# A new hand-written order for the first stage of a Flamingo block: loads, steps and the engines of its conversions

## The chip, the cores and the metric

The kernel runs on one core of a Trainium2 chip. The metric is the device time in microseconds (us) of one execution; lower is better. The core has a matrix engine (TensorE, called PE in the profile), three engines for element-wise work (VectorE or DVE, ScalarE or ACT, GpSimd or POOL), and SyncE (SP), which here issues nearly all DMA transfers. Each engine works through its own queue of instructions strictly in order, and an instruction that waits for another engine holds everything behind it on its own.

## The reference

Two batches of 512 tokens with 1024 features (`x`) and two contexts of 1024 x 1024 (`ctx`) come in. The first half of the block is an "attention" without a softmax: the normalised tokens and the context are each put on an integer grid of 256 steps, and multiplied.

```python
def fake_quant(x, s, z):
    q = clip(round(x / s + z), 0, 255)
    return (q - z) * s

x = x + tanh(g_xattn[0]) * (fake_quant(layernorm(x)) @ fake_quant(ctx))
x = x + tanh(g_ffn[0]) * ffn(layernorm(x))
```

`ffn` is a shared gated layer, `(silu(x @ sw1 + sb1) * (x @ sw2 + sb2)) @ sw3 + sb3`, with 512 inner features, plus experts of the same form with 256 inner features, of which a router (`x @ router_w`, a softmax, and the best two within the two best of four groups) picks two of 16 for each token.

## The kernel before

The 1024 tokens are eight tiles of 128; tiles 0 to 3 belong to batch 0 and tiles 4 to 7 to batch 1. The context of a batch has eight row blocks of 128. The work up to the first part of the shared layer is written out by hand as one long list of small steps, `START`, which a loop turns into instructions one after another. The order of the list is the order of every engine's queue; the tile framework adds the waits between engines. The loads ahead of it stand in a second list, `LOADS`, and all go through SP in that order.

```python
LOADS = "x.1 x.3 c.0 c.1 c.2 c.4 c.3 x.2 c.5 x.4 c.6 c.7.0 c.7.1 b x.5 w.0.0 w.1.1 w.1.0 w.0.1"
for step in START.split():
    name, *args = step.split(".")
    do[name](*(int(a) if a.isdigit() else a for a in args))
```

In `LOADS`, `x.t` is a token tile (512 KB), `c.k` a context block of batch 0 (512 KB; `c.7` comes in two halves), `b` the biases, `w.c.i` the weights of inner block c of the shared layer (i is 0 for `sw1`, 1 for `sw2`), 512 KB in rows of 128 numbers. `x.0` is loaded first, in two halves. In the profile, `X` is a token tile, `cr` a context block, and `sa0r`, `sb0r`, `sa1r`, `sb1r` are `w.0.0`, `w.0.1`, `w.1.0`, `w.1.1`.

A step names its operation, its tile or block, sometimes a half, and often the engine:

- token side, tile t: `bn` and `ag` take mean and variance (DVE, L205, L209); `qa`, `qp`, `qr` make scale and offset (`qp` is a power on POOL, L218); `qn` turns a sign for ACT; `q8` quantises to bytes (DVE L237, ACT L235); `qc` centres to bf16 (L190 on ACT, L192 elsewhere); `qt` transposes on PE (L248) into `pq`; `qe` copies that out into `qT`.
- context side, batch b, block k: `c8` quantises (ACT L261, others L263) and `cc` centres into `cq` (L190, L192). In the text c1.k is the load of block k of batch 1.
- `mm.t.k` multiplies transposed block k of tile t by context block k, into two accumulators `at` (PE, L273, two products of 512 columns; `mm.t.7.0` is one of them).
- `e` adds the result to the tile (DVE, L285); `sq` squares on ACT (L294); `fm`, `fc`, `fa`, `fr` make the second norm's mean and scale; `fn` applies it into `xn` (DVE, L323); `px` transposes on PE (L328); `xh`, `xl` split the transpose into a high part `XH` (L184, L186) and a low part `XL` (DVE, L338); `xc` makes a negated copy for the router (ACT).
- shared layer, weights `w.c.i`: `wh` takes the high part and `wl` the low part (L589); `um` is eight products of 256 columns on PE (L598) into `sp`; `us` and `ug` apply the gate (ACT L605, DVE L608).
- `ld` issues the eight context blocks of batch 1 and then `x.6` and `x.7`; `lw` issues three small DMAs for the router, its weights `rwf` (64 KB, L617), a bias `rb` of 16 numbers (L618) and a broadcast row `rbi` (L619); `xd` stores a tile, `lz` loads the next two weight blocks, `ud` stores a gated block. All of these are on SP.
- `kb.n` is n dummy products on PE (L570) ahead of the first real ones; `pw` makes four sums for the router on POOL (L672).

PSUM has six banks of one kind (`at`, `sp`, and `px` with `.m`) and two of another (`pq` and `px` without it); `q8`, `qc`, `c8` and the gated blocks rotate over seven buffers of SBUF. A step that needs a bank or a buffer waits for the last reader of the one that it takes over.

After `START` come the rest of the shared layer (L385), the router, the experts (L429) and the down projection (L978, L989), in which PE works from product to product.

Of the kernel before, what the change touches and what calls it, by code (L numbers as in the profile page):

```python
# [74 lines left out]


# [1173 lines left out]
```

## Time and profile before

| | |
|---|---|
| median of 3 runs | 307.93 us (307.24 to 308.5) |
| the profiled execution | 308.13 us |
| its span, first to last instruction | 306.4 us |
| PE busy | 296.7 us, 97% of the span |
| DVE, ACT, POOL busy | 217.4, 150.4, 88.3 us |
| the granted clock of TensorE | 0.999 of full speed |
| first PE instruction of the stage after `START` | 79.38 us after the span's start |

A line of a group or of the timeline has the engine, the line of the kernel, the operation, its output and inputs, shapes and types, and how often it came; in brackets, the idle time ahead of it and what ended that. A line of the waits tells who waited for whom: us in total, how often, the longest. A line of the chain has start, duration and what it was. "SPq" is SP's own queue of DMA issues: its durations are those of the issue, not of the transfer.

### The profile page before, as it was taken

To read this page: it belongs to the slowest core of one execution; us is meant where nothing else is said; L and a number is where in the kernel's file an instruction comes from. 1 tells how busy PE (TensorE), PEld (TensorE's weight loads), DVE (VectorE), ACT (ScalarE), POOL (GpSimd) and SP (SyncE) were. 2 spreads that over 40 slices of the span, in tenths; PEclk is the share of its full clock that TensorE was granted. 3 is DMA by queue.
4 is the path that set the end of the run, shared out by engine and by line. 5 is a ranking of instruction groups with operands and counts; after the bars stand their busy time and mean duration, and the time that the engine had idled before them with its cause. 6 is when DMAs were issued, how large, how long until landed. Compare 5 with 4: busy or idle time off the path is not lost.

```text
span 306.4 us, 4242 instructions
## 1 busy us (share of the span) xinstructions
PE 296.7 (97%) x1502; PEld 232.4 (76%) x1502; DVE 217.4 (71%) x371; ACT 150.4 (49%) x214; POOL 88.3 (29%) x118
## 2 busy tenths in 40 slices
PE   8889999999999999999999999999999999999993
PEld 3344794599858888888888888888888888888882
DVE  3999998996948599864572758725489597756522
ACT  2779999768252464453241544417663638420000
POOL 2567996659322312400011110212430050000000
PEclk9999999999999999999999999999999999999999
DMA  6999950982159972641504209049999999812222
GB/s 229 418 395 313 393 190 1 279 356 88 35 159 193 216 154 43 120 158 38 170 0 120 86 4 254 18 149 360 286 348 314 346 216 300 255 74 103 81 93 75
DMA packets 39553, 56.90 MB, mean 186 GB/s; under 512 B 5389, under 2 KB 22613, under 8 KB 39524
## 3 DMA queue, kind: packets, MB, share of 16 engines
q1 hardware_dynamic: 36194, 48.16, 45.6%
q0 software_dynamic: 3328, 8.39, 14.7%
q8 instruction: 14, 0.23, 0.3%
q14 instruction: 15, 0.12, 0.1%
q10 hardware_dynamic: 2, 0.00, 0.0%
HBM read 39.76 MB, written 12.59 MB: 171 GB/s over the span
## 4 chain that ended last, share of the span: by engine, by line
PE 81%; DMA 11%; SPq 3%; DVE 1%; POOL 1%; issue 0%; POOLq 0%
PE pb L978 11%; DMA X<-in_dram 9%; PE sp L385 7%; PE pa L978 7%; PE pc L978 6%; PE sp L598 4%; PE b2B L429 3%; PE b3B L429 3%; PE b7B L429 3%; PE b5B L429 3%; PE b4B L429 3%; PE b6B L429 3%; PE at L273 3%; DMA cr<-in_dram 2%; PE b6C L429 2%; PE b7C L429 2%
## 5 line engine op out<-in xcount | busy, mean ns | idle before, releaser
L273 PE MATMUL at<-cq,qT 128*128 128x512 bf16 x128 | 29.9, 379 | 1.3 <-POOL cq L192 1.0
L273 PEld LDWEIGHTS <-qT 128*128 128x128 bf16 x128 | 12.2, 98 | 14.9 <-issue 2.1
L989 DVE SCALAR_TENSOR_TENSOR Y<-pb,tg,Y 128x512 f32<-128x512 f32 x12 | 9.0, 749 | 8.6 <-PE pb L978 8.5
L825 POOL DMA_DIRECT2D xf<-xf x8 | 7.2, 938 | 23.3 <-DMA xf<-xf 13.4
L949 POOL DMA_DIRECT2D rS<-hrouted x6 | 7.3, 1601 | 21.9 <-DMA rS<-hshared 15.1
L570 PE MATMUL pz<-zero 128*128 128x512 bf16 x43 | 11.6, 421 | 1.5 <-DVE zero L563 1.5
L989 DVE SCALAR_TENSOR_TENSOR Y<-pc,tg,Y 128x512 f32<-128x512 f32 x8 | 5.9, 750 | 10.0 <-PE pc L978 10.0
L205 DVE BATCH_NORM_STATS2 st<-X 128x6 f32<-128x512 f32 x16 | 10.4, 675 | 3.5 <-DMA X<-in_dram 3.5
L461 POOL TENSOR_TENSOR b4s<-b4s,gates 128x512 f32<-128x512 f32 x2 | 2.6, 1288 | 35.1 <-ACT b4s L471 27.9
L285 DVE SCALAR_TENSOR_TENSOR X<-at,cx_scale,X 128x512 f32<-128x512 f32 x16 | 11.7, 744 | 0.1
L294 ACT ACTIVATE xn<-X,s 128x512 f32<-128x512 f32 x16 | 11.5, 718 | 0.0
L261 ACT ACTIVATE q8c<-cr,sc_in,rs 128x1024 uint8<-128x1024 f32 (+1 forms) x9 | 10.2, 1135 | 2.0 <-DMA cr<-in_dram 2.0
L190 ACT ACTIVATE cq<-q8c,nz 128x1024 bf16<-128x1024 uint8 (+1 forms) x10 | 10.4, 1057 | 1.2 <-DVE q8c L263 1.1
L338 DVE TENSOR_TENSOR XL<-px,XH 128x512 fp32r<-128x512 f32 x16 | 10.3, 679 | 0.5 <-ACT xf L345 0.5
L184 ACT CAST XH<-px 128x512 fp32r<-128x512 f32 x13 | 7.3, 607 | 5.6 <-PE px L328 5.6
L598 PE MATMUL sp<-XH,sb 128*128 128x256 f32 x64 | 9.6, 291 | 0.0
L672 POOL TENSOR_TENSOR xf<-XH,XL 128x1024 f32<-128x1024 f32 x4 | 9.5, 2411 | 0.0
L972 DVE TENSOR_TENSOR rB<-rB,rB 128x1024 f32<-128x1024 f32 x8 | 9.2, 1219 | 0.0
L570 PEld LDWEIGHTS <-zero 128*128 128x128 bf16 x43 | 4.2, 105 | 6.4 <-DVE zero L563 1.5
L328 PE MATMUL px<-ident,xn 128*128 128x128 f32 x64 | 8.8, 274 | 0.3 <-DVE xn L323 0.3
L598 PE MATMUL sp<-XH,sa 128*128 128x256 f32 x64 | 8.8, 286 | 0.0
L598 PEld LDWEIGHTS sp<-XH,sb 128*128 128x128 f32 x64 | 8.3, 191 | 0.4 <-ACT XH L184 0.2
(602 smaller groups left out, 889.2 us busy)
## 6 DMA issues: line engine op xcount, KB each, us to landing
cr<-in_dram SPq DMA_DIRECT2D x15, 512.0 KB, 8.5
x_after<-X SPq DMA_DIRECT2D x8, 512.0 KB, 7.2
xf<-xf POOLq DMA_DIRECT2D x8, 512.0 KB, 5.2
rB<-in_dram SPq DMA_DIRECT2D x8, 512.0 KB, 8.8
Y<-x_after SPq DMA_DIRECT2D x8, 512.0 KB, 8.7
out_dram<-Y SPq DMA_DIRECT2D x15, 256.0 KB, 2.1
X<-in_dram SPq DMA_DIRECT2D x7, 512.0 KB, 9.4
rS<-hrouted POOLq DMA_DIRECT2D x6, 512.0 KB, 11.5
```

The source lines that it names most:

```text
L190: nc.scalar.activation(out, q8, AF.Identity, bias=nz)
L205: nc.vector.bn_stats(st_[t][:, h, :], X[t][:, half(h)])
L273: nc.tensor.matmul(acc[t][h], qT[b][:, t % TB, k, :], cq[b][k // KH][:, k % KH, half(h)], start=(k == 0), stop=(k == KD - 1))
L285: nc.vector.scalar_tensor_tensor(xs, acc[t][h], cx_scale, xs, ALU.mult, ALU.add, accum_out=sq_[t][0][:, h : h + 1])
L294: nc.scalar.activation(xn_[t][:, half(h)], X[t][:, half(h)], AF.Square, bias=s[:, h : h + 1], scale=-float(H), accum_out=q[:, h : h + 1],)
L338: nc.vector.tensor_tensor(XL[b][q][p], px_[t, q], XH[b][q][p].bitcast(F32), ALU.subtract)
L385: nc.tensor.matmul(p, wx[:, k, :], xx[b][k // KH][:, k % KH, cols], start=first and k == 0, stop=last and k == KD - 1,)
L429: nc.tensor.matmul(p, w[:, k, :], x[:, k, :], start=f and k == 0, stop=l and k == KH - 1, skip_group_check=not first,)
L570: nc.tensor.matmul(pz[0], zero[:, :P], zero, start=True, stop=True)
L598: nc.tensor.matmul(up_[c, lo, i], w[:, k, :], x[0][k // KH][:, k % KH, lo : lo + 256], start=p == 0 and k == 0, stop=p == 2 and k == KD - 1,)
L978: nc.tensor.matmul(p, x[:, ts(t, P)], w[:, cl], start=first and k == 0 and i == 0, stop=k == KH - 1 and i == 2, skip_group_check=not first,)
L989: nc.vector.scalar_tensor_tensor(X[t][:, cl], p, tgf, X[t][:, cl], ALU.mult, ALU.add)
```

## The change

Only the two lists change. Every step is still there once, with the same arithmetic, and the 43 dummy products are too.

- `LOADS`: `x.2` goes ahead of `c.2`, and `x.4` behind all of batch 0's context; `c.3`, `c.4`, `c.6`, `c.5` swap places; `w.1.0` comes first of the weights, and `x.5` and `b` stand among them.
- `START`: of PE's steps, the first products start on tiles 0 and 1 as before, but tile 2 comes before tile 3; nearly all dummy products stand in one run ahead of the first transpose.
- `lw` moves from the middle of batch 1 to the front of the list, ahead of `ld`. `ld` itself moves up to the first part of the list; both are still behind all of `LOADS` on SP. `xd.0`, `xd.1` and `lz` follow directly behind `ld`.
- Some 55 steps go to another engine: for example `qc.0` from ACT and DVE to POOL, `c8.0.1` from ACT to POOL, `qc.1` from DVE to ACT, `c8.0.4` and `cc.0.4` from ACT to DVE, both halves of `c8.0.7` and `cc.0.7` from DVE and ACT to POOL, `wh.1.1.1` from DVE to ACT, `c8.1.1` and `c8.1.2` from POOL to ACT, `c8.1.0` from ACT to DVE, `qc.4` from ACT to POOL, `c8.1.6` and `cc.1.5` from ACT to DVE.

The diff in full:

```diff
@@ -39,38 +39,38 @@
 LOWEST = -3.4028234663852886e38
 
 
-LOADS = "x.1 x.3 c.0 c.1 c.2 c.4 c.3 x.2 c.5 x.4 c.6 c.7.0 c.7.1 b x.5 w.0.0 w.1.1 w.1.0 w.0.1"
+LOADS = "x.1 x.3 c.0 c.1 x.2 c.2 c.3 c.4 c.6 c.5 c.7.0 c.7.1 x.4 w.1.0 w.0.0 x.5 b w.1.1 w.0.1"
 START = """
-kb.4 ks bn.0.0 bn.0.1 ag.0 qa.0.dve kr kn xx.0 qp.0 kb.8 kb.1 qr.0.dve kb.3 q8.0.dve.0 kx kz qc.0.act.0 stage.0 kb.7
-qt.0.0 bn.1.0 bn.1.1 bn.3.0 ag.1 bn.3.1 ag.3 qa.1.pool c8.0.0.act.0 qp.1 q8.0.dve.1 qa.3.dve qc.0.dve.1 cc.0.0.act.0
-kb.2 qr.1.pool c8.0.1.act c8.0.0.dve.1 cc.0.1.act kb.3 q8.1.dve qc.1.dve kb.7 qt.0.1 qe.0.dve.0 qp.3 kb.3 c8.0.2.act
-qr.3.pool kb.4 qt.1 q8.3.dve cc.0.0.pool.1 mm.0.0 qe.1.dve cc.0.2.pool c8.0.5.pool mm.0.1 qc.3.act qe.0.dve.1
-c8.0.3.dve kb.1 mm.1.0 mm.1.1 qt.3 cc.0.3.dve mm.1.2 bn.2.0 bn.2.1 c8.0.4.act qe.3.act mm.0.2 ag.2 cc.0.4.act bn.4.0
-bn.4.1 c8.0.6.dve mm.0.3 mm.3.0 cc.0.5.act mm.3.1 qa.2.pool qp.2 c8.0.7.dve.0 cc.0.7.dve.0 mm.1.3 cc.0.6.act mm.3.2
-mm.1.4 mm.3.3 mm.1.5 qr.2.pool c8.0.7.act.1 mm.0.4 mm.0.5 ld ag.4 pb q8.2.dve mm.1.6 qc.2.pool bn.5.0 cc.0.7.act.1
-mm.1.7.0 mm.0.6 bt mm.3.4 wh.0.0.0.act qa.4.dve mm.1.7.1 qt.2 e.1.0 mm.3.5 mm.0.7.0 e.1.1 mm.0.7.1 mm.3.6 sq.1.0
-qe.2.dve e.0.0 sq.1.1 wh.0.0.1.act qp.4 e.0.1 qr.4.pool bn.5.1 fm.1.pool sq.0.0 fm.0.dve ag.5 fc.1.pool fc.0.dve
-qa.5.dve mm.2.0 mm.2.1 wl.0.0.0.pool sq.0.1 mm.2.2 fa.1.pool wh.1.0.0.act fa.0.dve mm.2.3 mm.2.4 fr.1 wh.1.1.0.dve
-fn.1.0 fr.0 mm.2.5 mm.2.6 mm.2.7.0 mm.3.7.0 fn.1.1 px.1.0.m fn.0.0 px.1.1.m fn.0.1 qp.5 e.3.0 px.0.0 c8.1.0.act
-qn.4.dve mm.2.7.1 xh.1.0.act xh.1.1.act wh.1.1.1.dve xh.0.0.act xl.1.0 xl.1.1 c8.1.1.pool wh.0.1.0.dve px.0.1
-wh.0.1.1.dve xl.0.0 mm.3.7.1 wl.0.0.1.pool xh.0.1.act stage.1 q8.4.act xl.0.1 qc.4.act e.2.0 qr.5.pool c8.1.3.act
-um.1.0.1.0 um.0.0.0.0 wl.1.0.0.dve um.0.0.1.0 qt.4 e.3.1 wh.1.0.1.act um.0.0.1.1 c8.1.2.pool c8.1.4.pool q8.5.dve
-qe.4.dve cc.1.3.act e.2.1 cc.1.1.act wl.0.1.0.pool wl.0.1.1.dve cc.1.4.pool um.0.0.0.1 um.1.0.1.1 fm.3.pool um.1.0.0.0
-cc.1.0.pool um.0.0.0.2 qc.5.act bn.6.0 c8.1.6.act bn.7.0 bn.7.1 cc.1.2.act c8.1.7.act um.0.0.1.2 ag.7 qt.5 bn.6.1
-qa.7.dve c8.1.5.pool qe.5.dve us.0.0 ag.6 qa.6.dve um.1.0.0.1 qp.7 qr.7.pool mm.4.0 ug.0.0 lw mm.4.1 sq.2.0 cc.1.5.act
-qn.7.dve mm.4.2 mm.4.3 mm.5.0 mm.5.1 cc.1.6.dve mm.5.2 fm.2.pool mm.5.3 mm.4.4 fc.2.dve mm.5.4 q8.7.act sq.3.0
-wl.1.0.1.dve mm.5.5 qp.6 mm.5.6 cc.1.7.dve qc.7.act qr.6.pool mm.5.7 q8.6.dve qc.6.dve mm.4.5 qt.7 sq.2.1 e.5.0 qt.6
-fa.2.pool qe.7.act e.5.1 mm.4.6 mm.4.7 xd.5 fm.5.dve e.4.0 fr.2 mm.7.0 mm.7.1 fc.3.dve sq.3.1 fa.3.dve sq.5.0 fr.3
-qe.6.act e.4.1 mm.7.2 fm.4.pool mm.7.3 mm.7.4 mm.7.5 fn.3.1 sq.4.0 fn.2.1 fn.3.0 mm.7.6 sq.5.1 mm.6.0 fc.5.pool mm.6.1
-lz wl.1.1.0.dve mm.7.7 px.3.1 mm.6.2 xh.3.1.act fa.5.pool mm.6.3 fr.5 mm.6.4 px.2.1 fc.4.pool e.7.0 xd.1 mm.6.5 sq.4.1
-mm.6.6 rc xh.2.1.act fn.2.0 e.7.1 fm.7.pool fn.5.1 mm.6.7 fn.5.0 sq.7.0 xl.3.1 px.2.0.m e.6.0 px.3.0.m xd.0 fc.7.pool
-um.1.0.0.2 wl.1.1.1.pool sq.7.1 xh.3.0.act e.6.1 xx.1 sq.6.0 px.5.1.m xh.2.0.act fm.6.dve xc.5.1 xl.3.0 ud.0.0
-fc.6.pool px.5.0 um.1.0.1.2 xl.2.1 fa.4.pool sq.6.1 fr.4 um.1.256.0.0 fa.7.dve xh.5.1.act xl.2.0 um.0.256.0.0
-xh.5.0.dve fa.6.pool um.1.256.0.1 xl.5.1 fn.4.0 fr.7 fn.7.0 fr.6 px.4.0 us.1.0 px.7.0.m xh.7.0.act fn.7.1 xc.5.0 xd.4
-um.0.256.0.1 um.1.256.0.2 fn.4.1 us.1.256 px.4.1.m fn.6.1 fn.6.0 xd.2 px.6.0.m xc.7.0 xc.6.0 xc.4.0 xl.5.0 ug.1.0
-um.0.256.0.2 px.6.1 xh.6.1.dve xh.4.0.act xl.4.0 xl.6.1 um.1.256.1.0 xd.6 pw xl.7.0 xh.4.1.act xh.6.0.act um.1.256.1.1
-um.1.256.1.2 px.7.1 um.0.256.1.0 um.0.256.1.1 xd.7 xc.4.1 xc.6.1 ud.1.0 ug.1.256 um.0.256.1.2 xd.3 xh.7.1.dve us.0.256
-xl.4.1 xc.7.1 xl.6.0 xl.7.1 ud.1.256 ug.0.256 ud.0.256
+kb.4 ks bn.0.0 bn.0.1 kb.8 kb.1 ag.0 lw kx kr c8.0.0.act.0 c8.0.0.act.1 qa.0.pool qp.0 qr.0.dve kb.3 kz q8.0.dve.0
+kb.7 kn kb.2 bn.1.0 bn.1.1 ag.1 ld stage.0 qa.1.dve kb.3 kb.7 bn.3.0 qc.0.pool.0 qp.1 qr.1.dve c8.0.1.pool
+cc.0.0.act.1 q8.0.dve.1 qc.0.pool.1 kb.3 kb.4 q8.1.dve bn.3.1 bn.2.0 bn.2.1 qt.0.0 qc.1.act ag.2 qe.0.act.0
+cc.0.0.pool.0 c8.0.2.act qt.1 ag.3 qa.2.dve qe.1.dve c8.0.3.act mm.0.0 cc.0.1.dve qa.3.pool kb.1 cc.0.3.act qt.0.1
+cc.0.2.dve mm.1.0 qe.0.act.1 qp.2 mm.0.1 mm.1.1 qr.2.pool c8.0.4.dve q8.2.dve mm.1.2 qc.2.act mm.1.3 mm.0.2 qp.3
+c8.0.6.dve cc.0.6.act mm.0.3 cc.0.4.dve qr.3.pool c8.0.7.pool.0 cc.0.7.pool.0 qt.2 c8.0.5.dve c8.0.7.pool.1 mm.0.4
+mm.1.4 qe.2.dve mm.2.0 cc.0.5.act q8.3.dve mm.1.5 qc.3.act mm.1.6 mm.0.5 xx.0 bn.4.0 cc.0.7.pool.1 bn.4.1 wh.1.0.0.dve
+mm.1.7.0 e.1.0 wh.1.0.1.act qt.3 ag.4 mm.0.6 mm.0.7.0 qe.3.act sq.1.0 mm.0.7.1 qa.4.dve mm.2.1 wl.1.0.1.pool e.0.0
+e.0.1 mm.2.2 mm.1.7.1 qp.4 wh.0.0.0.act sq.0.0 sq.0.1 e.1.1 mm.2.3 mm.2.4 mm.2.5 qr.4.dve mm.3.0 wh.1.1.0.dve
+fm.0.pool mm.3.1 mm.3.2 fm.1.pool pb fc.0.dve qn.4.dve bn.5.0 wh.0.0.1.dve fc.1.pool fa.0.pool bn.5.1 sq.1.1
+wh.0.1.0.act mm.3.3 mm.3.4 bt fr.0 q8.4.act fn.0.0 mm.3.5 fa.1.pool px.0.0 fn.0.1 ag.5 fr.1 px.0.1 fn.1.1 mm.2.6
+mm.2.7.0 px.1.1.m fn.1.0 mm.2.7.1 xh.0.0.act c8.1.0.dve xh.0.1.act qa.5.pool px.1.0.m xh.1.1.act xh.1.0.act
+wh.0.1.1.dve e.2.0 wl.0.1.1.pool xl.1.1 mm.3.6 xl.0.1 xl.1.0 xl.0.0 qc.4.pool c8.1.2.act mm.3.7.1 qp.5 e.2.1
+wl.1.0.0.dve c8.1.1.act wl.0.1.0.dve sq.2.0 qr.5.dve c8.1.4.pool wh.1.1.1.act q8.5.dve xd.0 mm.3.7.0 um.1.0.0.0 e.3.0
+fm.2.pool um.0.0.1.0 qt.4 c8.1.3.act um.0.0.0.0 stage.1 e.3.1 bn.6.0 wl.0.0.0.pool wl.0.0.1.pool cc.1.4.act xd.1
+um.1.0.1.0 qe.4.dve cc.1.3.act bn.6.1 lz bn.7.0 cc.1.0.pool ag.6 um.1.0.0.1 sq.2.1 qa.6.dve um.1.0.0.2 cc.1.2.act
+um.0.0.1.1 bn.7.1 xd.3 ag.7 um.0.0.0.1 fc.2.dve um.0.0.1.2 qc.5.act qa.7.dve c8.1.5.pool c8.1.6.dve um.0.0.0.2
+cc.1.1.act cc.1.5.dve mm.4.0 qp.7 qt.5 qr.7.pool um.1.0.1.1 mm.4.1 c8.1.7.act qn.7.dve us.0.0 mm.4.2 mm.4.3 qe.5.dve
+sq.3.0 fa.2.pool mm.4.4 fr.2 qp.6 q8.7.act ug.0.0 mm.5.0 fn.2.0 qr.6.dve cc.1.7.dve mm.5.1 mm.5.2 qc.7.act q8.6.dve
+cc.1.6.dve mm.4.5 mm.5.3 rc mm.5.4 qt.7 qc.6.act fm.3.pool mm.4.6 sq.3.1 mm.4.7 wl.1.1.1.pool mm.5.5 wl.1.1.0.dve
+qe.7.dve qt.6 mm.5.6 e.4.0 e.4.1 us.1.0 fm.4.pool mm.5.7 e.5.0 mm.7.0 mm.7.1 sq.5.0 px.2.0.m mm.7.2 mm.7.3 fn.2.1
+fc.3.dve qe.6.dve xd.2 e.5.1 mm.7.4 px.2.1 sq.5.1 fa.3.pool mm.6.0 xh.2.0.act sq.4.0 fr.3 mm.7.5 mm.7.6 fm.5.dve
+fc.5.pool fn.3.0 mm.7.7 mm.6.1 fa.5.pool xh.2.1.act mm.6.2 fn.3.1 mm.6.3 fr.5 e.7.0 px.3.0.m mm.6.4 fn.5.1 xl.2.0
+px.3.1 xh.3.0.act mm.6.5 xh.3.1.act e.7.1 xl.2.1 sq.4.1 xx.1 fn.5.0 sq.7.0 px.5.1.m fm.7.pool sq.7.1 mm.6.6 fc.7.pool
+fc.4.dve px.5.0 xl.3.0 xl.3.1 xd.7 um.1.256.0.0 mm.6.7 fa.7.dve e.6.0 um.1.256.0.1 um.1.0.1.2 xc.5.1 fr.7 fa.4.pool
+um.0.256.1.0 fr.4 fn.7.0 sq.6.0 um.0.256.0.0 e.6.1 fm.6.dve xh.5.1.act ud.0.0 sq.6.1 fc.6.dve fn.4.0 px.7.0.m
+um.1.256.0.2 fn.4.1 xd.5 xl.5.1 fa.6.dve xc.5.0 px.4.0 px.4.1.m um.0.256.0.1 fr.6 fn.6.1 xd.6 xh.5.0.act us.1.256
+xh.4.0.act fn.6.0 fn.7.1 um.0.256.1.1 xc.4.0 xl.5.0 xh.4.1.dve px.7.1 xc.4.1 px.6.0.m ug.1.0 xl.4.0 pw xh.7.0.act
+um.0.256.0.2 xh.7.1.dve ud.1.0 xh.6.0.act xl.6.0 xc.7.1 um.1.256.1.0 px.6.1 xc.6.1 xl.7.1 xl.7.0 um.1.256.1.1 us.0.256
+xc.6.0 xh.6.1.dve xd.4 um.1.256.1.2 xl.6.1 ug.1.256 um.0.256.1.2 xc.7.0 ug.0.256 ud.0.256 ud.1.256 xl.4.1
 """
 
 
```

## The prediction

> **What bounds the kernel now.** I read the page first: busy shares, then the chain that ended last.
>
> ```profile
> PE 296.7 (97%) x1502; PEld 232.4 (76%) x1502; DVE 217.4 (71%) x371; ACT 150.4 (49%) x214; POOL 88.3 (29%) x118
> ...
> PE 81%; DMA 11%; SPq 3%; DVE 1%; POOL 1%; issue 0%; POOLq 0%
> ```
>
> TensorE is the bound; DMA holds the chain only early. So I asked for the waits of PE alone (total us, times, longest), then PE's timeline.
>
> ```profile
> PE pz L570 <- DVE zero L563: 1.5, 1, 1.5
> PE pq L248 <- DVE qx L192: 1.3, 3, 0.5
> PE at L273 <- POOL cq L192: 1.0, 1, 1.0
> PE px L328 <- DVE xn L323: 0.3, 1, 0.3
> PE pq L248 <- ACT qx L190: 0.2, 1, 0.2
> PE at L273 <- DVE sa L608: 0.2, 1, 0.2
> ```
> ```profile
> 16.63 0.81 PE L273 MATMUL at<-cq,qT 128*128 128x512 bf16 x3 [1.01 <-POOL cq L192]
> ...
> 31.81 1.63 PE L328 MATMUL px<-ident,xn 128*128 128x128 f32 x12 [0.27 <-DVE xn L323]
> ...
> 34.12 1.39 PE L598 MATMUL sp<-XH,sb 128*128 128x256 f32 x8
> ...
> 79.38 2.00 PE L385 MATMUL sp<-XH,sa 128*128 128x512 f32 x8
> ```
>
> START ends at 79.38; from there the chain is PE alone up to the last addition. In START, PE waits 1.5 for its first operand (untouched) and 3.0 in all the rest. The change keeps every PE step, the 43 dummy products too. So it can win at most 3.0 us, and loses what new waits exceed that. Last I read the chain's loads, the DMA by stretch (last numbers: clock, DMA share, GB/s), and SP:
>
> ```profile
> 26.61 6.14 DMA cr<-in_dram
> ...
> 32.77 11.19 DMA X<-in_dram
> ```
> ```profile
> 26.00:28.00 2.00, 2.00 (x17) 1.13 (x16) 1.94 (x6) 2.00 (x6) 1.71 (x7) 1.00 1.05 290
> ...
> 38.00:40.00 2.00, 2.00 (x19) 2.00 (x18) 2.00 (x4) 2.00 (x4) 2.00 (x2) 1.00 1.02 418
> 40.00:42.00 2.00, 2.00 (x19) 2.00 (x19) 2.00 (x5) 1.48 (x2) 2.00 (x2) 1.00 1.01 338
> 42.00:44.00 2.00, 2.00 (x21) 1.84 (x20) 1.69 (x5) 2.00 (x3) 1.90 (x5) 1.00 0.25 33
> ```
> ```profile
> 34.07 0.38 SPq L617 DMA_DIRECT2D rwf<-in_dram  x1
> 35.31 3.54 SPq L618 DMA_DIRECT2D rb<-in_dram  x1
> 38.90 1.12 SPq L619 DMA_DIRECT2D rbi<-in_dram  x1
> ```
>
> The load stream is full from 2 to 42 us: c1.1 lands at 32.75, x.7 at 43.96. Summing bytes of 2 us stretches, x.4 (eleven half-MB loads, 5.77 MB) has moved by 17.25 and lands at 19.20: landing is about 1.95 after moving. A load of 4 KB rows takes 1.25 (0.524 MB at 420 GB/s). From x.5 (7.38 MB, 21.3) to the fourth weight half (9.48 MB, 28.0) is 6.7 us, so a half takes 1.68.
>
> **The change, part by part.** I walk each engine's new queue in order with durations of the trace.
>
> *Loads.* x.2 moves up, x.4 down: x.2 lands at 12.95, c.7 at 20.4 (21.7 before), x.4 at 21.8, w.1.0 23.5, w.0.0 25.2, x.5 26.4, w.1.1 28.2, w.0.1 30.0. The total up to the second context is unchanged.
>
> *lw ahead of ld.* Three DMAs (64 KB router weights in rows of 64 bytes, 64 bytes of biases, one broadcast row) move past all eight c1 loads, x.6 and x.7, on SP and in the rings. Row: in 40:44 the 0.74 MB moved take until about 42.8; the 0.68 MB of large rows need 1.6 us from 40, so the small ones hold the engines about 1.2. [...] c1.2 lands at 35.6, x.6 near 43.8, x.7 at 45.2. SP's issue time is taken as hidden: SP comes to lw near 26.5, the rings are full of weights to 28.0; without that cover see the first rival.
>
> *First products.* PE runs 42 dummies in a row to 12.7 (0.217 each at the end). c8.0.0 goes whole to ACT (c.0 lands 10.46): two halves and cc.0.0's half at 0.72-0.81, to 12.7; qc.1 (1.15) follows to 13.8; qt.1 runs at 13.9, qe.0 on ACT (half of 1.01), first product 14.35 (15.24 before, its second half 16.63). New waits of PE up to qt.3: 1.0 for qc.1, then 0.1, 0.25 (cc.0.1 on DVE), 0.5 (cc.0.3 behind c.3, landed 15.45), 0.4 (qc.2), 0.45 (qe.2 behind c8.0.5), 0.1. qt.3 ends at 23.8; before, the same work was done at 24.1 (32 products and three transposes at 24.36; 3 x 0.217 less, one transpose of 0.44 more). Gain 0.3.
>
> *Swapped engines.* Some 55 small and large steps change engine, at like prices: a 1024-wide conversion is 1.06-1.23 on ACT, 0.75-0.81 on DVE, 1.1-1.33 on POOL. What can differ is DVE beside POOL:
>
> ```profile
> 18.26 1.57 DVE L192 TENSOR_SCALAR cq<-q8c,nz 128x1024 bf16<-128x1024 uint8 x1
> ...
> 47.62 0.74 DVE L192 TENSOR_SCALAR cq<-q8c,nz 128x1024 bf16<-128x1024 uint8 x1
> ```
>
> The first runs beside a POOL conversion (18.07 to 19.29), the second beside small POOL steps. POOL gets c8.0.1, qc.0, half of cc.0.0 and all of c.7; DVE gets c8.0.4 and c8.0.5. No stretch of before has this mix: between nothing and 0.8 for each of three overlaps. I take 0.3 in all, which goes into the waits below.
>
> *px.0.0.* PE comes to it at 29.7. On DVE before fn.0.0: e.0.0 from 24.6, three e at 0.75 to 26.85, qr.4, then wh.1.1.0 waits for w.1.1 (28.2); behind it fc.0, qn.4, two bn (0.61), wh.0.0.1, fn.0.0: px.0.0 at 31.2. New wait 1.5 (0.27 before). With w.1.1 early it would be 0.5. [...] First um at 34.8 instead of 34.12, where the first eight themselves run 0.3 slow: loss 0.4.
>
> *um.1.0.1.0, fourth of its kind.* It needs wh.1.1.1, moved to ACT behind c8.1.2, c8.1.1 and sq.2.0: 35.6 + 1.23 + 1.15 + 0.9 + 0.6 = 39.5. PE, after 0.5 for qt.4 (qc.4 now on POOL behind wl.0.1.1), is there at 38.8: wait 0.7. With the loads as before, wh.1.1.1 would end at 38.5: none. Seven um of 0.97 then lead to mm.4.0 at 46.3.
>
> *mm.5.0.* It needs qe.5 and banks that ug.0.0 frees. DVE: bn.6.0 waits for x.6, then qe.4, bn.6.1, bn.7, ag, fc.2, c8.1.6, cc.1.5 and qn.7 (behind qr.7 on POOL) stand before qe.5: 49.8, ug.0.0 50.3. PE is there at 49.85: wait 0.4 (0.2 before).
>
> *Buffers.* q8, qx and c8 rotate over seven buffers; I followed each reuse in the new order, and every earlier reader is done when the next writer comes (c8.0.5, the tightest, needs cc.0.2, done 1.5 earlier). Nothing; if one binds, its conversion is late by up to one of 0.8 to 1.2.
>
> *Later.* Transposes of tiles 2 to 7, their squares and the stores keep about one PE step of slack by the walk; xd.0, xd.1 and lz now stand on SP directly behind the loads and move by about 51 (four halves of a MB, 1.25 to 1.68 each, after 45), in rings that are idle from 42 to 53; the four POOL sums of pw (9.5) end near 82, needed at 86. Nothing, but see the third rival.
>
> Sum on PE from qt.3: -0.3 at the front, then waits of 1.5 + 0.5 + 0.7 + 0.4 = 3.1. Before had from there 0.27 + 0.19 + 0.32, 0.3 in the slow first um, and 0.15 of pipeline restart at each of three stops (a product of 512 columns counts 0.379 and they follow at 0.217): 1.5. With the new stops' restarts already in the starts: -0.3 + 3.1 - 1.5 = +1.3. Against the profiled execution (308.13, span 306.4) 309.4; it stands 0.2 over the median 307.93, so 309.2.
>
> **The rivals.**
>
> *SP is held (slower).* rb's issue took 3.54 and rbi's 1.12 behind rwf. If they take that in the new place as well, from 26.6, c1.0 is issued near 31.3; the rings run dry at 29.2, and it moves 2.5 later still. It decides once rb and rbi end later than about 28.7. c1.2, wh.1.1.1 and x.7 shift by 2.5 and PE has nothing else: +3.8, 311.7. For it: these rows. Against: in 35 to 39 the rings were full, and the two DMAs are tiny.
>
> *The front pays (faster).* w.1.1 lands by 27.2 and lw costs near its bytes: px.0.0 waits 0.5, wh.1.1.1 and x.7 cause nothing. Then 1.0 + 0.7 + 0.3 go from the sum: -0.7, 307.2; with the overlaps at nothing and the early waits halved, -2.0. For it: earlier c.7 and tile 2. Against: before is within 3.0 of its floor.
>
> *A stop near the end (slower).* xh.2.0 now stands on ACT behind sq.5.1, and px.3.0 needs a bank from e.7.0 or xl.2.0: slack 0.4. If it is gone, one or two stops of 0.8 are added: 310.5.
>
> **How the numbers follow.** Main course 0.55, SP held 0.17, the front pays 0.20, late stop 0.08. 0.5% is 1.54 us, about what a measurement of this kernel can tell from no change. The main course, 1.3 with 1.0 to each side (308.2 to 310.2 is its own range), is past 1.54 in four of ten: 0.22; with SP held and three quarters of the late stop, slower is 0.45. Faster by over 0.5% is a quarter of the front's case and a little of the main one: 0.07. The rest, 0.48, is within. Forecast 309.2. The range leaves out the fastest third of the front's case and the upper third of SP held: 306.9 to 311.4.
>
> **What would show it.** Right: PE's waits have px near 1.5 behind DVE xn, and sp behind the cast wh.1.1.1 (ACT) about 0.7; rwf is issued ahead of c1.0; x.7 lands near 45.2; the first L385 starts at 80.7; behind it all is unchanged. Wrong: x.7 at 44 and no wait of sp (lw free); c1.0 issued after 30 and stops of 2 to 3 us (SP held); first L385 before 79 (the front pays); stops after 60 us.

## The result, and the profile after

The changed kernel is slower: 310.45 us (median of 6 runs, 309.97 to 312.85) against 307.3 us for the kernel before (6 runs beside them). The ratio is 1.0114, 95% interval 1.0074 to 1.0155: about 3.5 us, with the lower end already outside the 0.5% of "no change". The profiled execution took 310.07 us, 1.94 more than that of before; its span is 308.4 us against 306.4. The readings below explain those 2.0 us, not all of the 3.5. The profiled execution of before (308.13) is itself 0.8 above the median beside it, and that of the changed kernel 0.4 below its own; both make the difference in the profiles smaller. Two of the six executions of the changed kernel, 312.07 and 312.85, have a mean granted clock of 0.989 and 0.994, where the other four have 0.996 to 0.999; what held those two back no trace shows.

First, what TensorE waited for in the changed kernel (waits of PE: total us, times, longest):

```profile
PE at L273 <- DVE qT L186: 1.7, 1, 1.7
PE pz L570 <- DVE zero L563: 1.5, 1, 1.5
PE at L273 <- ACT cq L190: 0.5, 1, 0.5
PE b2C L429 <- DVE b2s L491: 0.4, 1, 0.4
PE px L328 <- DVE xn L323: 0.2, 1, 0.2
...
```

The early stops of before for `qx` and `cq` are nearly gone. In their place stands one stop of 1.7, and a new one at L429, a line that belongs to the experts, well behind `START`. PE's timeline places them:

```profile
30.30 1.08 PE L328 MATMUL px<-ident,xn 128*128 128x128 f32 x8 [0.23 <-DVE xn L323]
...
33.93 1.19 PE L598 MATMUL sp<-XH,sa 128*128 128x256 f32 x8 [0.16 <-DVE X L285]
...
37.39 1.44 PE L598 MATMUL sp<-XH,sb 128*128 128x256 f32 x8
...
49.92 2.92 PE L273 MATMUL at<-cq,qT 128*128 128x512 bf16 x12 [1.70 <-DVE qT L186]
...
80.57 2.00 PE L385 MATMUL sp<-XH,sa 128*128 128x512 f32 x8
...
127.26 1.19 PE L429 MATMUL b2C<-S4h,b2b 128*128 128x512 f32 x4 [0.42 <-DVE b2s L491]
```

The first `um` starts at 33.93, 0.2 ahead of before (34.12). All of the loss in `START` comes later, most of it at mm.5.0 (49.92). The first L385 starts at 80.57 instead of 79.38: 1.19 lost. From there to the end of the span it is 227.8 us, before 227.0: 0.8 more is lost behind `START`, in code that the change does not touch. So there are two losses with two places, 1.2 and 0.8.

SP and the load stream, in the changed kernel (SP's queue of issues; then DMA by stretch, last numbers clock, DMA share, GB/s):

```profile
22.74 2.97 SPq L617 DMA_DIRECT2D rwf<-in_dram  x1
25.76 1.40 SPq L618 DMA_DIRECT2D rb<-in_dram  x1
27.20 0.42 SPq L619 DMA_DIRECT2D rbi<-in_dram  x1
27.66 4.26 SPq L531 DMA_DIRECT2D cr<-in_dram  x8
```
```profile
26.00:28.00 2.00, 2.00 (x11) 0.93 (x10) 1.96 (x10) 2.00 (x6) 1.52 (x7) 1.00 0.96 221
28.00:30.00 2.00, 2.00 (x11) 0.80 (x9) 1.78 (x4) 1.88 (x5) 1.64 (x5) 1.00 0.61 61
```

The same two views of the kernel before, for SP's issue of the c1 loads and for the second stretch:

```profile
24.72 6.48 SPq L531 DMA_DIRECT2D cr<-in_dram  x8
```
```profile
28.00:30.00 2.00, 2.00 (x11) 0.90 (x10) 1.96 (x7) 2.00 (x6) 1.74 (x4) 1.00 1.09 360
```

In 26 to 28 the DMA engines are busy (0.96) but move only 221 GB/s, where before moved 290. In 28 to 30 they are busy for 0.61 of the time and move 61 GB/s, where before moved 360: the queue has run short while SP is still coming to the first c1 load, whose issue begins at 27.66 (24.72 before). From 30 to 32 it moves 408 GB/s. The last load lands accordingly, as DVE's timeline shows; the same view has what follows it up to qe.5 (L186):

```profile
44.85 0.69 DVE L205 BATCH_NORM_STATS2 st<-X 128x6 f32<-128x512 f32 x1 [1.00 <-DMA X<-in_dram]
...
46.81 0.81 DVE L263 TENSOR_SCALAR q8c<-cr,rs,sc_in 128x1024 uint8<-128x1024 f32 x1
...
49.11 0.15 DVE L227 TENSOR_SCALAR qb<-qb 128x1 f32<-128x1 f32 x1 [0.83 <-POOL qb L223]
49.18 0.68 DVE L186 COPY qT<-pq 128x1024 bf16<-128x1024 bf16 x1
```

In DVE's timeline of before, the line of x.7 reads:

```profile
43.98 1.29 DVE L205 BATCH_NORM_STATS2 st<-X 128x6 f32<-128x512 f32 x2 [0.31 <-DMA X<-in_dram]
```

x.7 lands at 44.85 (43.98 before). Five microseconds of DVE and POOL work stand between it and the end of the copy that PE waits for, and part of that is a wait of DVE for POOL. POOL's `qp.7`, one power on 128 numbers, took 1.35 there; before, `qp.7` took 0.56, and `qp.6` had the 1.35.

Last, the second loss. What stands at the seam behind `START`, in POOL's timeline and then DVE's:

```profile
72.52 9.80 POOL L672 TENSOR_TENSOR xf<-XH,XL 128x1024 f32<-128x1024 f32 x4
...
97.77 0.86 POOL L825 DMA_DIRECT2D xf<-xf  x1 [5.33 <-DMA xf<-xf]
```
```profile
81.83 1.56 DVE L356 TENSOR_TENSOR b2al<-sa2r,b2ah 128x1024 fp32r<-128x1024 f32 x1
...
112.62 1.23 DVE L356 TENSOR_TENSOR S2l<-xf,S2h 128x1024 fp32r<-128x1024 f32 x1 [1.21 <-ACT S2h L355]
```

And in the kernel before, POOL's and then DVE's:

```profile
69.88 9.48 POOL L672 TENSOR_TENSOR xf<-XH,XL 128x1024 f32<-128x1024 f32 x4
...
95.11 0.86 POOL L825 DMA_DIRECT2D xf<-xf  x1 [3.85 <-DMA xf<-xf]
```
```profile
79.98 1.22 DVE L356 TENSOR_TENSOR b2al<-sa2r,b2ah 128x1024 fp32r<-128x1024 f32 x1
```

The four sums of `pw` (L672) run from 72.52 to 82.32, so they end 1.75 behind the first L385; before they ran from 69.88 to 79.36 and ended with it. DVE's first subtraction behind `START`, `b2al`, takes 1.56 (1.22 before) beside them and starts 0.7 later against PE. Behind it hang a load (`sa3r`) and then POOL's accumulating transfers (L825): the second pair waits 5.33 (3.85 before), `S2l` then waits 1.21, and `b2s` reaches PE 0.42 late.

### The profile page after: what moved, and what is told of

The parts are those of the page before. It is cut to its first block, busy times and chain, and to the rows that moved or that the text cites. A ratio compares the mean times of both kernels' runs of the same rounds, so it can differ in the third digit from the quotient of the medians.

```text
span 308.4 us, 4232 instructions
## 1 busy us (share of the span) xinstructions
PE 297.9 (97%) x1496; PEld 232.7 (75%) x1502; DVE 218.1 (71%) x375; ACT 148.1 (48%) x212; POOL 89.5 (29%) x116
## 4 chain that ended last, share of the span: by engine, by line
PE 79%; DVE 5%; POOL 5%; ACT 3%; DMA 3%; issue 2%; SPq 1%; POOLq 0%; DVEq 0%
PE pb L978 11%; PE sp L385 7%; PE pa L978 7%; PE pc L978 6%; PE sp L598 4%; PE at L273 3%; PE b7B L429 3%; PE b6B L429 3%; PE b5B L429 3%; PE b4B L429 3%; PE b3B L429 3%; DMA cr<-in_dram 2%; PE b2C L429 2%; PE b2B L429 2%; PE b7C L429 2%
## 5 line engine op out<-in xcount | busy, mean ns | idle before, releaser
L570 PE MATMUL pz<-zero 128*128 128x512 bf16 x43 | 12.5, 456 | 1.5 <-DVE zero L563 1.5
L825 POOL DMA_DIRECT2D xf<-xf x8 | 7.2, 936 | 23.4 <-DMA xf<-xf 12.7
L261 ACT ACTIVATE q8c<-cr,sc_in,rs 128x1024 uint8<-128x1024 f32 (+1 forms) x8 | 8.7, 1127 | 5.6 <-DMA cr<-in_dram 5.6
L672 POOL TENSOR_TENSOR xf<-XH,XL 128x1024 f32<-128x1024 f32 x4 | 9.8, 2479 | 0.0
L328 PEld LDWEIGHTS px<-ident,xn 128*128 128x128 f32 x64 | 7.5, 140 | 2.2 <-issue 0.7
L323 DVE TENSOR_SCALAR xn<-X,nm,d 128x512 f32<-128x512 f32 x16 | 8.2, 543 | 1.2 <-POOL d L319 1.2
L598 PE MATMUL sp<-XH,sb 128*128 128x256 f32 x64 | 8.9, 284 | 0.1
```

What stands on the lines that cost most here:

```text
L328: nc.tensor.transpose(px_[t, q][:, k, :], xn_[t][:, ts(4 * q + k, P)], ident)
L570: nc.tensor.matmul(pz[0], zero[:, :P], zero, start=True, stop=True)
L598: nc.tensor.matmul(up_[c, lo, i], w[:, k, :], x[0][k // KH][:, k % KH, lo : lo + 256], start=p == 0 and k == 0, stop=p == 2 and k == KD - 1,)
```

## The experiments

All were timed beside the kernel before, e3 and e4 in 6 executions and the others in 12. For each, the profiled execution gives: the span, the start of the first L385, the time from there to the end, and when `pw` ends against the first L385.

| | ratio to before, 95% interval | span | first L385 | behind it | `pw` ends |
|---|---|---|---|---|---|
| before | | 306.4 | 79.38 | 227.0 | 0.0 |
| changed | 1.0114 (1.0074 to 1.0155) | 308.4 | 80.57 | 227.8 | +1.8 |
| e1: lw back | 1.0038 (1.0009 to 1.0067) | 307.1 | 79.61 | 227.5 | +1.7 |
| e2: lw alone | 1.0042 (1.0012 to 1.0071) | 307.2 | 80.23 | 227.0 | 0.0 |
| e3: qe.5 up | 1.0133 (1.0074 to 1.0192) | 308.7 | 80.99 | 227.7 | +1.8 |
| e4: xl.4.1 up | 1.0123 (1.0070 to 1.0176) | 309.8 | 81.38 | 228.4 | +1.8 |
| e5: e1, qe.5 and qp.6 up | 1.0007 (0.9983 to 1.0032) | 307.2 | 79.06 | 228.1 | +1.8 |
| e6: e1's first half, then before's | 1.0014 (0.9988 to 1.0040) | 306.4 | 79.43 | 227.0 | +0.3 |
| e7: before's first half, then changed | 1.0033 (1.0004 to 1.0062) | 306.8 | 79.56 | 227.2 | +1.7 |
| e8: e5's first half, then before's | 1.0013 (0.9993 to 1.0033) | 306.4 | 79.49 | 226.9 | +0.3 |
| e9: e7, `pw` earlier | 0.9994 (0.9963 to 1.0025) | 306.0 | 79.00 | 227.0 | +0.1 |
| e10: e5, `pw` earlier | 0.9996 (0.9964 to 1.0028) | 307.1 | 80.07 | 227.0 | +0.1 |
| e11: rwf alone ahead of ld | 0.9983 (0.9955 to 1.0012) | 306.6 | 79.57 | 227.0 | 0.0 |
| e12: rb, rbi alone ahead | 1.0028 (0.9994 to 1.0063) | 308.5 | 81.60 | 226.9 | 0.0 |

**What lw costs (e1, e2).** e1 is the changed kernel with this one step put back behind the loads, e2 the kernel before with this one step put ahead of them.

```diff
 e1, in the changed START:
-kb.8 kb.1 ag.0 lw kx kr
+kb.8 kb.1 ag.0 kx kr
-bn.1.1 ag.1 ld stage.0
+bn.1.1 ag.1 ld lw stage.0
 e2, in the START of before:
-mm.0.4 mm.0.5 ld ag.4
+mm.0.4 mm.0.5 lw ld ag.4
-mm.4.0 ug.0.0 lw mm.4.1
+mm.4.0 ug.0.0 mm.4.1
```

> The changed kernel with one step moved: lw directly behind ld, so that the router's three small DMAs stand behind x.7 again. Theory 1 (the loss in START comes from lw ahead of the second context): no gap in the load stream near 28 us, x.7 lands by 43.5 instead of 44.85, the 1.70 us wait for qe.5 falls below 0.6, the first L385 starts near 79.4 instead of 80.57, and the time falls by 1.0 to 1.7 us. Rival 2 (the loss is the order of DVE's and POOL's steps between bn.7 and qe.5): x.7 lands earlier all the same, but the wait stays above 1.2 and the time falls by 0.4 us at most.

> The kernel before with one step moved: lw directly ahead of ld. Theory 1: a gap in the load stream near 28 us, x.7 lands 0.9 to 1.5 us later than 43.96, the first L385 starts 0.6 to 1.2 us later than 79.38, and the time rises by as much. Rival 2: the loads come later but the steps behind them have room; the first L385 moves by less than 0.3 us and the time by less than 0.4.

Putting lw back takes the ratio from 1.0114 to 1.0038, and the intervals do not meet. Its profile has no gap (330 and 346 GB/s in the two stretches), x.7's statistics start at 43.90 with no wait for the load, and the stop at mm.5.0 shrinks from 1.70 to 0.47:

```profile
48.95 2.92 PE L273 MATMUL at<-cq,qT 128*128 128x512 bf16 x12 [0.47 <-DVE qT L186]
```

The same edit moves something else: SP issues the first stores (`xd`) at 40.38 instead of 34.48. No run moves them alone, but e2, where no store stands there, has its last load late too. In the kernel before, lw alone costs 0.42%; the gap is there in full, and the last load is 0.9 late (44.84). Stretches of e2:

```profile
26.00:28.00 2.00, 2.00 (x16) 1.05 (x15) 1.93 (x6) 2.00 (x6) 1.74 (x5) 1.00 0.97 243
28.00:30.00 2.00, 2.00 (x11) 0.88 (x9) 2.00 (x7) 2.00 (x6) 1.81 (x4) 1.00 0.52 43
```

The time is lost by another load than in the changed kernel, though. The list of before converts c1.0 on ACT, and the casts of XH that the first `um` needs stand behind that conversion. ACT's timeline of before, then of e2, then PE's of e2:

```profile
30.78 1.24 ACT L261 ACTIVATE q8c<-cr,sc_in,rs 128x1024 uint8<-128x1024 f32 x1 [0.40 <-DMA cr<-in_dram]
```
```profile
32.33 1.24 ACT L261 ACTIVATE q8c<-cr,sc_in,rs 128x1024 uint8<-128x1024 f32 x1 [1.58 <-DMA cr<-in_dram]
```
```profile
35.07 1.22 PE L598 MATMUL sp<-XH,sb 128*128 128x256 f32 x8 [0.40 <-ACT XH L184]
```

In e2, e7, e9, e11 and e12, which share this part of the list, the first `um` starts 2.73 or 2.74 behind that conversion, so a late c1.0 is what PE pays. The changed list converts c1.0 on DVE and pays by x.7. Of the 0.85 that e2's first L385 is late, 0.36 stood there at 15 us (tile 1's transposes at 15.15 against 14.79), before lw was issued at 23.87; the trace leaves about 0.5 for lw.

So lw is the largest single cost found in the change. It costs time in the list of before too, by another path.

**Which of lw's three DMAs (e11, e12).** `lw` was split in two: the 64 KB with rows of 64 bytes (`rwf`) on one side, the two tiny ones (`rb`, `rbi`) on the other. Both kernels are the kernel before with one part moved.

```diff
     def lw():
         nc.sync.dma_start(rwf[:, :, :E], rw.rearrange("(k p) e -> p k e", p=P))
+
+    def lv():
         nc.sync.dma_start(rb4[:E], rvec[0:E].unsqueeze(1))
         nc.sync.dma_start(rbi, rvec[E : 2 * E].partition_broadcast(P))
 e11: ... mm.0.5 lw ld ag.4 ...   and lv where lw was
 e12: ... mm.0.5 lv ld ag.4 ...   and lw where it was
```

> The kernel before with only the first of the three DMAs of lw (rwf, 64 KB in rows of 64 bytes) directly ahead of ld; rb and rbi stay where they were. Theory of the prediction (the cost is the time that the engines need for the many small rows): the stream still falls below 250 GB/s in 26 to 30, x.7 lands 0.8 to 1.0 later than before's 43.98, the first L385 0.6 to 0.9 later, ratio 1.003 to 1.004, nearly all of what the three cost together. Rival (SP is held by the issue of rb and rbi, and the rings run dry meanwhile): the stream stays above 280 GB/s in both stretches, x.7 within 0.3 of before, ratio 1.000 to 1.001.

> The other part: the kernel before with only rb (16 numbers) and rbi (a broadcast row) directly ahead of ld; rwf stays where it was. Theory of the prediction (small rows on the engines): hardly a dent in the stream, x.7 within 0.2 of 43.98, ratio within 0.001 of 1. Rival (SP held): the issue of rb takes 1.4 to 3.5 at this place, the stream falls below 250 GB/s behind it, x.7 0.6 or more late, ratio 1.003 to 1.004.

Neither theory got its numbers. Either part alone opens a hole of the same size in 28 to 30: 166 GB/s at a share of 0.83 with rwf, 164 at 0.84 with rb and rbi, against 360 with neither and 43 with both (e2). In both, c1.0 is issued late, at 26.92 and at 26.34 (24.72 before, 28.17 in e2); with rb and rbi ahead, where almost no extra bytes move, `rb`'s issue took 1.48 and `rbi`'s 0.42. So the late issue alone could explain all of these holes, though no run separates it; and no run shows that the 64-byte rows of rwf cost the DMA engines something of their own here. In time, rwf alone is level with before, against the prediction's theory, and rb with rbi is unclear: the interval reaches from 0.9994 to 1.0063. How the 0.42% divides stays open, and so does why c1.0 was there for ACT only at 33.28 in e12, 2.5 later than before, when it was issued 1.6 later. The profiled execution of e12 shows what a hole can do when a load arrives late enough. ACT's timeline, then PE's:

```profile
33.28 1.24 ACT L261 ACTIVATE q8c<-cr,sc_in,rs 128x1024 uint8<-128x1024 f32 x1 [3.97 <-DMA cr<-in_dram]
```
```profile
36.01 1.51 PE L598 MATMUL sp<-XH,sb 128*128 128x256 f32 x8 [3.01 <-ACT XH L184]
37.32 1.91 PE L598 MATMUL sp<-XH,sa 128*128 128x256 f32 x8
```

ACT waits 4.0 for c1.0, the casts of XH that PE needs stand behind that conversion on ACT's queue, and PE stops for 3.0. The first L385 is 2.2 late.

**The chain behind x.7 (e3, e5).** e3 moves tile 5's copy and the gate ahead of qn.7, the step of tile 7 on DVE that waits for POOL, in the changed kernel; e5 does the same on e1, and also takes qp.6 ahead of tile 7's small POOL steps and fn.2.0 behind cc.1.6.

```diff
 e3 and e5:
-qt.5 qr.7.pool um.1.0.1.1 mm.4.1 c8.1.7.act qn.7.dve us.0.0 mm.4.2 mm.4.3 qe.5.dve
+qt.5 qe.5.dve qr.7.pool um.1.0.1.1 mm.4.1 c8.1.7.act us.0.0 ug.0.0 qn.7.dve mm.4.2 mm.4.3
-q8.7.act ug.0.0 mm.5.0
+q8.7.act mm.5.0
 e5 also:
-sq.2.1 qa.6.dve um.1.0.0.2
+sq.2.1 qa.6.dve qp.6 um.1.0.0.2
-mm.4.4 fr.2 qp.6 q8.7.act
+mm.4.4 fr.2 q8.7.act
-mm.5.0 fn.2.0 qr.6.dve
+mm.5.0 qr.6.dve
-cc.1.6.dve mm.4.5
+cc.1.6.dve fn.2.0 mm.4.5
```

> The changed kernel with qe.5 directly behind qt.5, and us.0.0, ug.0.0 ahead of qn.7, so that DVE no longer waits for POOL's qr.7 with qe.5 behind it. Rival 2 in its simple form (the wait of qn.7 is what PE pays): qe.5 is done near 49.0 instead of 49.86, mm.5.0 starts 0.9 earlier, START ends 0.9 earlier, time -0.9 us. Theory 1 in its strict form (everything behind x.7 is one chain over bn.7, qa.7, qp.7, qr.7, fr.2, qp.6, qr.6, q8.6, cc.1.6 to mm.4.6 at 53.38): mm.5.0 starts earlier but PE then waits for cc.1.6 instead, START ends at most 0.3 earlier, time unchanged within 0.4.

> The changed kernel with lw directly behind ld again, and with three moves around x.7: qe.5 ahead of qa.7, us.0.0 and ug.0.0 ahead of qn.7, and qp.6 with fn.2.0 placed so that tile 6 does not queue behind tile 7's small POOL steps. Theory 1 (one chain behind x.7 on DVE and POOL feeds both qT of tile 5 and cq of the last contexts, so moving one copy alone only hands the stop on; moving the POOL step of tile 6 as well shortens the chain itself): no stop of PE over 0.3 at mm.5.0 or mm.4.6, the first L385 near 78.9 against 79.6 with lw moved alone, time ratio near 1.001. Rival (the chain is set by x.7's arrival and DVE's total work, not its order): the stop moves on as before, the first L385 stays at 79.5 to 79.9, ratio 1.004 or more.

(Where e5's text has qe.5 ahead of qa.7, the edit has it ahead of qn.7, still behind qa.7.)

e3 frees mm.5.0 and gains nothing, because the stop moves on to the next consumer of the same chain, tile 4's product with cq.1.6. Its PE timeline:

```profile
49.42 2.92 PE L273 MATMUL at<-cq,qT 128*128 128x512 bf16 x12 [0.55 <-DVE qT L186]
...
53.80 1.24 PE L273 MATMUL at<-cq,qT 128*128 128x512 bf16 x5 [0.80 <-DVE cq L192]
```

The copy was only the first piece of a queue that starts at x.7. Counted from tile 7's first statistics on DVE (44.85 in the changed kernel, 43.90 in e1, 45.33 in e3, 45.67 in e4), the first L385 comes 35.7 later in all four, whatever stops PE had before. In e5 cq.1.6 is ready 7.5 behind these statistics (43.81) instead of 8.4 to 8.5, and the first L385 comes 35.25 behind them: the shorter chain is worth about 0.45. L385 starts at 79.06, 0.55 ahead of e1 and 0.3 ahead of before. The second stop is gone, though e1 had none there either, and the stop at mm.5.0 (0.55) is still there, against the expectation of at most 0.3. Of the time, e1 and e5 have 1.0038 and 1.0007 with intervals that meet, so the gain rests on the trace.

**The two halves (e6, e7).** Both lists hold the same steps, so a list can be cut at mm.7.0 (about 58 us) and continued with what is missing, in the other kernel's order and on its engines.

```diff
 e6: (changed, lw back) fm.4.pool mm.5.7 e.5.0
+e.5.1 xd.5 fm.5.dve mm.7.0 mm.7.1 fc.3.dve fa.3.dve sq.5.0 fr.3 qe.6.act   (and so on, order of before)
 e7: (before) fm.5.dve e.4.0 fr.2
+xd.0 xd.1 lz um.1.0.0.2 xd.3 fn.2.0 rc sq.3.1 wl.1.1.1.pool wl.1.1.0.dve   (and so on, order of the change)
```

> The changed list with lw behind ld up to mm.7.0 (about 58 us), and from there the remaining steps in the order and on the engines of the kernel before. Theory (part of the loss comes from the second half of the list: the four sums of pw on POOL begin 1.7 to 2.6 later, end after the first L385 and stretch DVE's last subtraction and the load and the sums behind it): pw begins by 70.7, the time from the first L385 to the end is 227.0 instead of 227.5, PE waits nowhere at L429, ratio 1.001 to 1.002. Rival (what follows START is late only because START's first half is): pw still begins near 71.5, the end stays 227.5 behind the first L385, ratio 1.004 as with the changed second half.

> The other half: the kernel before up to mm.7.0, and from there the remaining steps in the changed kernel's order and on its engines; loads and lw as before. Theory (the second half alone costs 0.5 behind START): first L385 within 0.3 of 79.4, pw begins 1.5 or more later than 69.9, 227.5 from the first L385 to the end, a wait of 0.3 to 0.4 at L429, ratio about 1.0015 to 1.002. Rival (the second half is harmless by itself): pw begins by 70.3, 227.0 from the first L385 to the end, no wait at L429, ratio 1.000.

With before's second half, what is behind `START` is 227.0, `pw` ends 0.3 behind the first L385 and the second pair of xf waits 3.80, although the first half is the changed one. With the changed second half `pw` ends 1.7 behind it and that pair waits 5.56, although the first half is that of before. So the late `pw` and the wait behind it belong to the second half of the list. What they cost over 227.0 differs: 0.2 in e7, 0.5 in e1, 0.8 in the changed kernel, 1.1 in e5, 1.4 in e4. The expectation for e7 was right in direction, not in size: 227.2 instead of 227.5, with a late `b2C` but no stop long enough to be listed.

**The cause of that loss (e4, e9).** e4 makes DVE start `b2al` earlier against PE by taking xl.4.1 from the end of the list; e9 also takes what `pw` waits for forward, on e7.

```diff
 e4, e9 and e10:
-um.1.256.1.2 xl.6.1 ug.1.256 um.0.256.1.2 xc.7.0 ug.0.256 ud.0.256 ud.1.256 xl.4.1
+um.1.256.1.2 xl.6.1 xl.4.1 ug.1.256 um.0.256.1.2 xc.7.0 ug.0.256 ud.0.256 ud.1.256
 e9 and e10 also:
-sq.6.1 fc.6.dve fn.4.0 px.7.0.m um.1.256.0.2 fn.4.1
+sq.6.1 fc.6.dve fa.6.dve fr.6 fn.4.0 px.7.0.m um.1.256.0.2 fn.4.1 fn.6.1 fn.6.0
-xl.5.1 fa.6.dve xc.5.0 px.4.0 px.4.1.m um.0.256.0.1 fr.6 fn.6.1 xd.6 xh.5.0.act us.1.256 xh.4.0.act fn.6.0 fn.7.1
+xl.5.1 xc.5.0 px.4.0 px.4.1.m um.0.256.0.1 xd.6 xh.5.0.act us.1.256 xh.4.0.act fn.7.1
```

> The changed kernel with DVE's last step of START, xl.4.1, ahead of ug.1.256. The first L385 stays at 80.6. Theory 3 (the rest of the loss comes after START: DVE leaves START 0.7 us later against PE than before, the loads of the next weights start later and meet POOL's accumulating DMAs, the splits S2 are late and PE waits for b2C): DVE starts b2al 0.6 earlier, the DMAs xf on POOL run at 2.5 to 3 us each, the 0.4 us wait of b2C goes, time -0.4 to -0.8 us. Rival (those DMAs vary from run to run by themselves): b2al is earlier and the time is unchanged within 0.3.

> The kernel before up to mm.7.0 and the changed second half, as in the run before the last, with three moves: fa.6 and fr.6 directly behind fc.6, fn.6.1 and fn.6.0 directly behind fn.4.1, and xl.4.1 ahead of ug.1.256. Theory (the loss behind START is the late pw on POOL: DVE's last subtraction runs beside it, so the load of sa3r is issued late, in front of the accumulating transfers of xf, and the splits fed by them reach PE late): pw begins near 70.1 instead of 71.4 and ends by 80.0, sa3r is issued about 1 us earlier against the first L385 (7.1 instead of 8.0), the second pair of xf waits 3.9 instead of 5.6, L429 runs with no wait, 227.0 instead of 227.2 to 227.4 behind the first L385, ratio 1.0015 to 1.002. Rival (the loss behind START is something else in the changed half, such as its order of banks and of the last stores): pw is early and the second pair of xf still waits over 5, ratio 1.003 as before the moves.

e4's theory fell, and its DVE timeline says why:

```profile
82.12 2.10 DVE L356 TENSOR_TENSOR b2al<-sa2r,b2ah 128x1024 fp32r<-128x1024 f32 x1
```

The subtraction starts 0.74 behind the first L385 instead of 1.26, and takes 2.10 instead of 1.56: POOL's sums run until 83.14, and it ends no earlier against PE. In all six kernels with a late `pw` (changed, e1, e3, e4, e5, e7), `b2al` ends 1.07 to 1.09 behind the last of the sums, wherever it started, and in all fourteen kernels `sa3r` is issued 5.2 to 5.3 behind `b2al`. So the end of `pw` sets that issue. In e9, where `pw` is early, POOL's timeline reads:

```profile
69.47 9.65 POOL L672 TENSOR_TENSOR xf<-XH,XL 128x1024 f32<-128x1024 f32 x4
...
95.18 0.86 POOL L825 DMA_DIRECT2D xf<-xf  x1 [4.32 <-DMA xf<-xf]
```

`b2al` is back at 1.22, the second pair of xf waits 4.32 instead of 5.56, nothing at L429 is late, and 227.0 is left behind L385. e7 and e9 share their first half and differ by these five moved steps; the ratios are 1.0033 and 0.9994, but their intervals overlap, so this too rests on the traces. The plainer pair is e5 and e10, which differ by the same five: `pw` ends 0.1 behind the first L385 instead of 1.8, the second pair of xf waits 3.94 instead of 5.76, the stop of 0.41 at L429 is gone, and 227.0 is left instead of 228.1.

The moves have a price in `START`. The first sum now runs beside DVE's fn.7.1, which took 0.49 in the changed kernel. DVE's timeline of e10:

```profile
71.05 2.15 DVE L323 TENSOR_SCALAR xn<-X,nm,d 128x512 f32<-128x512 f32 x1
```

It took 2.15 in e9 as well, and PE loses about 0.5 at the transposes that follow: e10 is 0.48 behind e5 at 70.67 and 1.01 behind it at the first L385.

Across the table the split is clean: with `pw` ending 1.7 or more behind the first L385, 227.2 to 228.4 follow; with 0.3 or less, 226.9 to 227.0. That the second pair waits because its transfers run into the load of `sa3r` fits the issue times (1.8 us between the two issues where the wait is long, 2.4 to 2.7 where it is short), but no run separated it from the lateness itself.

**All together (e8, e10).** e8 is e5's first half with before's second, e10 is e5 with e9's moves.

> Changed list with lw behind ld and the three moves around x.7 up to mm.7.0, the order of the kernel before from there. If the two theories hold and add up: first L385 near 78.9, 227.0 behind it, ratio 0.998 to 1.000, so the changed first half with its faults removed is at best level with the kernel before. If either falls: ratio 1.002 to 1.004.

> The changed kernel with lw directly behind ld, the three moves around x.7 and the three moves near the end of START. If all three theories hold and add: first L385 near 79.0, 227.0 behind it, span 306.1, ratio 0.998 to 1.000, level with the kernel before or a hair ahead. If the moves near the end only shift the stop: first L385 at 79.0 to 79.4, 228 behind it, ratio 1.001 to 1.002.

With the faults removed the changed list is level with before, and no better: 1.0013 and 0.9996. Behind `START` both have 227.0 or 226.9 as expected. Within it e8 lies at 79.49 and e10 at 80.07, not near 79. Of the 1.0 between e10 and e5, half was there at mm.5.0 (48.94 against 48.46), with the same list up to there, and half is the price named above. No run is faster than the kernel before by more than its interval.

## Why the prediction was partly right

The time lay in the predicted range, and the direction of the likeliest case was right. Its size was not: +1.3 was forecast and +1.94 stands in the profiled executions, some 3.5 by the ratio, so the outcome given the highest chance, within 0.5%, did not happen; slower by more did. That the time stayed inside the range was in part luck: its upper part had been left for another case, SP held for long, and the loss behind `START` had been put at nothing.

- *At most 3.0 to be won, and nothing won.* Right. The front gain was there (first `um` 0.2 earlier) and was given back in full.
- *First products.* The dummy products ran to about 13.9, not 12.7, and covered the 1.0 of waiting for qc.1 that had been put behind them. The first product came at 14.98 (14.35 forecast, 15.24 before).
- *px.0.0, 1.5.* Measured 0.23. The mechanism was right and its size is no constant: the cast wh.1.1.0 waits for w.1.1 in some executions and not in others. In the changed kernel it ran at 27.27 with no wait (28.2 forecast for the landing). In e1, e3, e6 and e10 it waited 0.74, 1.14, 1.26 and 1.34, and PE then 0.75, 1.15, 1.27 and 1.43. DVE's timeline of e10:

```profile
28.52 0.43 DVE L186 CAST sb<-sb1r 128x512 fp32r<-128x512 f32 x1 [1.34 <-DMA sb1r<-in_dram]
```

  Why w.1.1 lands earlier in one execution than in another is open.
- *um.1.0.1.0, 0.7 behind the cast on ACT.* The chain was right: c1.2, c8.1.2, c8.1.1, sq.2.0, wh.1.1.1. The wait was about 0.3 (a group of 1.44 where its neighbours take 1.12), because c1.2 was converted from 34.44 and not 35.6. (Without lw the prediction's own terms give 38.3, not 38.5; no wait either way.)
- *mm.5.0, 0.4.* This is the mis-sized term inside `START`: 1.70. The start itself was put near 50.3 and came at 49.92, with qe.5 ended at 49.86 (49.8 forecast) and x.7 at 44.85 (45.2). PE went on with qe.5 and did not wait for ug.0.0, which ended at 50.25. What failed is where PE would be: the two stops ahead of it were smaller, so PE came earlier and waited for the same event. Here the chain that begins at the late load fixed a point in time (the first L385 came 35.7 behind tile 7's first statistics in four kernels), and the stops ahead of it did not add to it, they were taken from its wait. That is why the sum for `START` was nearly right, 1.19 against 1.3, with three terms wrong.
- *lw, 1.2 us of the engines, taken for SP's issue as hidden.* The delay was nearly right: the last load is 0.9 late in e2. (The prediction's row gives 0.9 too: a share of 0.25 from 42 to 44 ends at 42.5, not 42.8.) The reason was not: SP's issue was not hidden. SP came to lw at 22.74, not 26.5, rwf's issue took 2.97, and c1.0 was issued at 27.66. That is the rival "SP is held" in a mild form: rbi's issue ended at 27.6, short of the 28.7 from which that rival was to decide, and the queue ran short all the same (61 GB/s in 28 to 30). e11 and e12 show a hole of the same size for each part (166 and 164 GB/s in 28 to 30), so they do not show what the small rows cost the DMA engines by themselves.
- *"Later ... Nothing, but see the third rival."* This step failed. It had `pw` ending near 82, which is where it ended (82.32), and called that harmless because its result is needed at 86. The cost was not in the result: it was DVE's subtraction beside it, and the load and the transfers queued behind that. 0.8 in the profile.
- *The rivals.* "The front pays" did not come, since mm.5.0 took the gain. "A stop near the end" did not come at its place: PE has no wait over 0.2 between mm.5.0 and the first L385.

## What to carry to other kernels

Three small transfers ahead of a stream of loads moved the issue of its first load from 24.72 to 28.17 here (e2), and the stream from 360 to 43 GB/s in 28 to 30. Put such transfers behind the stream if nothing needs them early, and find out which late load the matrix engine then waits for: it was another one in each of the two lists here. When a stop is set by a late load and the queue behind it, freeing the first consumer can just move the stop to the second (e3: 0.55 and 0.80 in place of 1.70): count the whole chain from the load, and the stops ahead of it as parts of the same wait. When work moves later on an engine that is off the path, ask not only when its result is needed but what runs beside it at its new place (`b2al` took 1.56 instead of 1.22), and follow what hangs on that into the next stage. Moving it back earlier only helps if nothing worse stands beside it there (fn.7.1 took 2.15 instead of 0.49).
